# The last product of each scan block: from one VectorE instruction out of PSUM to a ScalarE copy and a GpSimd product

## The chip, the cores and the metric

The kernel runs on one core of a Trainium2 chip. The time is device microseconds (us) of one execution; three runs of the kernel before gave 946.91, 949.45 and 950.11, so their median is 949.45. A separate execution was profiled: 943.15 us, of which 941.0 lie between its first and its last instruction (the span). TensorE (PE) multiplies matrices into banks of PSUM; VectorE (DVE), ScalarE (ACT) and GpSimd (POOL) work elementwise; SyncE (SP) issues most of the DMAs. Each engine takes its own instructions in order.

## The reference

The computation is four layers, each normalised and added to x. Only the first, a Mamba block, matters here, and in it the lines from the scan to the output:

```python
def step(state, inp):
    dt_t, B_t, C_t, u_t = inp
    dA = jnp.exp(dt_t[..., None] * A)
    state = state * dA + (dt_t * u_t)[..., None] * B_t[:, None, :]
    y = jnp.einsum('bdn,bn->bd', state, C_t)
    return (state, y)
...
y = ys.transpose(1, 0, 2) + x * D
y = y * jax.nn.silu(gate)
return y @ W_out.T
```

There are 2 batches, 512 positions, 1024 channels and 16 states per channel. Then come a feed-forward layer with 4-bit weights, an attention layer and a mixture layer.

## The kernel before

The channels lie on the partitions, 128 at a time, and time runs along the free dimension. So there are 16 **blocks** (batch b, channel group c; `order[k]` in L1067), each a 128x512 tile in every quantity. A block takes 8 **steps**, one for each pair of states (`gi`); the main loop (L1152) runs over 128 steps `s = 8k + gi` and three more to drain. In step s:

- ScalarE computes the decays of step s+2 (`exps`, L1076) into one of two PSUM tiles `das`, which is free once the scan of step s has read it;
- VectorE forms du times B for step s+1 (`times_B`, L1092) and runs the recurrence of step s (`scan`, L1096);
- GpSimd multiplies the states with C (`times_C`, L1102) and, in 16 of the steps of batch 1, adds the pair up (L1104);
- TensorE adds the products of step s-2 into the bank of y (`sums`, L1124), with the identity as weights. The first matmul of a block (L1119, `gi == 0`, run in the step with gi = 2 of the next count) starts the bank with u times D.

The pool `ps_y` has one bank (L685), so y of the next block begins only when y of this one has been read. The reading is `fin(k)` (L1127), called at the head of the step with gi = 2 of the next block, that is s = 8k + 10: one VectorE product of the gate tile `g` with y, in place in `g`.

The same stage also carries other work as generators. `stream()` yields TensorE's matmuls one by one into what is free of 3.5 us per step: the gates, the in-projection of batch 1, then `out_tiles` (L978), which multiplies the finished `g` of batch 0 with W_out and starts when `st["fin7"]` is set, then the feed-forward layer of batch 0 (`ffn0`). In the steps with gi = 2 the stream's part comes before the sums, otherwise mostly after. Jobs started with `spawn(job, lag)` run in one of two `tick()`s per step; a job that puts a large product on GpSimd first takes `pool_turn()` (L181), of which there is one per step. The Softplus that makes dt of the next block (`dt_job`, L573) runs as such a job in the second tick of the step with gi = 1, ahead of that step's exps.

`pin()` (L407), called at the end of every step, fixes the order of instructions on TensorE, ScalarE, VectorE and GpSimd to the order in which they were traced. SyncE's queue is not pinned so. `jrow` hands out 128x512 tiles in SBUF from three slots. After the stage come the output projection of batch 1 (L1213) and the unpacking of the last weights (`once`).

Of the kernel before, what the change touches and what calls it, by code (L numbers as in the profile page):

```python
# [56 lines left out]
def tile_sandwich(  # L57
# [5 lines left out]
    nc = tc.nc  # L63
# [114 lines left out]
    scans, now = [], [0]  # L178
    pool_at = [-9]

    def pool_turn():  # L181

        while pool_at[0] == (now[0] - 1) // 2:
            yield 1
        pool_at[0] = (now[0] - 1) // 2
# [242 lines left out]
    with ExitStack() as mamba:  # L428
# [15 lines left out]
        def jrow(name):  # L444
            return jp.tile([P, S], F32, tag="j", name=name)
# [8 lines left out]
        g = [[None] * NCH for _ in range(B)]  # L454
# [13 lines left out]
        st = {}  # L468
# [214 lines left out]
        with ExitStack() as p2:  # L683
# [24 lines left out]
            def spawn(gen, lag=0):  # L708
                jobs.append([now[0] + lag, gen])
# [417 lines left out]
            def fin(k):  # L1127

                b, c = order[k]
                nc.vector.tensor_mul(g[b][c], g[b][c], st["y"])  # L1130
                st[f"fin{k}"] = now[0]

            def dt_job(k, ps):
                dt_out(*order[k], ps)
# [17 lines left out]
            for s in range(NS + 3):  # L1152
                k, gi = divmod(s, NGI)
# [3 lines left out]
                if gi == 2 and k:  # L1157
                    fin(k - 1)
# [39 lines left out]
        with ExitStack() as p3:  # L1198
# [9 lines left out]
            for j in range(NCH // 2):  # L1208
                w = wo_pair(1, 0, j)
                for e in range(2):  # L1210
                    c = 2 * j + e
# [305 lines left out]
```

## Time and profile before

| what | value |
|---|---|
| median of three runs | 949.45 us |
| profiled execution | 943.15 us |
| its span | 941.0 us |
| scan stage (steps 0 to 127) | about 66 to 567 us of the span |
| C product L1102, GpSimd, 128x1024 | 2362 ns, x128 |
| scan L1096, VectorE, 128x1024 | 2279 ns, x128 |
| B product L1092, VectorE, 128x1024 | 1205 ns, x127 |
| exps L1076, ScalarE, 128x511 | 691 ns, x256 |
| product of `fin` L1130, VectorE, 128x512 from PSUM | 666 ns, x16 |
| silu's product L727, GpSimd, 128x512 | 1269 ns, x15 for the gates |
| copy of dt L1084, ScalarE, 128x512 | 579 ns, x15 |
| load of an activation table, ScalarE | 1283 ns |

In a profile's groups each line names the source line, the engine, the operation, its output and inputs, their shapes, how often, the busy time with the mean of one, and after the bar the idle time just before, with the releaser that ended most of it. In a timeline the columns are start, duration, engine, line, operation and operands; in brackets stand the idle time before it and the releaser. Rows of busy time by stretch give the stretch, its length, busy time and number of records of each engine, TensorE's granted clock, the DMA share and GB/s. A matmul of fp32 operands, 128x512, shows as two records.

### The profile page before, as it was taken

What the parts mean: (1) busy time and instruction counts of PE and PEld (TensorE: products, weight loads), DVE (VectorE), ACT (ScalarE), POOL (GpSimd) and SP (SyncE); (2) the same over time, 40 slices, a digit from 0 to 9 for tenths busy, and PEclk for the clock granted to TensorE, in tenths of its full rate; (3) what the DMA queues carried; (4) which work ended last, traced back from release to release, by engine and by line L of the source; (5) the groups of instructions that cost most, each with busy time, mean ns of one, the idle gap of its engine ahead of it and who ended that gap; (6) DMA issues with size and microseconds to landing.
All of it is one profiled execution on the core that took longest, in us unless ns stands there. A gap on an engine that the chain in (4) does not pass through costs nothing.

```text
span 941.0 us, 7171 instructions
## 1 busy us (share of the span) xinstructions
PE 860.5 (91%) x2188; PEld 385.9 (41%) x2188; DVE 669.7 (71%) x770; ACT 428.3 (46%) x654; POOL 486.1 (52%) x356
## 2 busy tenths in 40 slices
PE   6989979879999898699999989899999998999994
PEld 3434433323544343244444434344544444445441
DVE  5778999999999998999999995525600034535235
ACT  3368875665667645656666530215320014322122
POOL 7758887767887777777788884520000000011012
PEclk9989999989999999799999999999999999999998
DMA  6549100110004954101110022356223121200101
GB/s 196 207 136 373 37 35 31 38 38 23 23 25 158 300 161 157 40 1 45 45 45 24 16 68 101 128 143 201 59 64 90 59 90 45 67 12 24 55 0 45
DMA packets 43816, 80.08 MB, mean 85 GB/s; under 512 B 7774, under 2 KB 20937, under 8 KB 43778
## 3 DMA queue, kind: packets, MB, share of 16 engines
q1 hardware_dynamic: 41506, 73.64, 24.0%
q0 software_dynamic: 1984, 5.47, 1.6%
q10 hardware_dynamic: 288, 0.52, 0.2%
q8 instruction: 17, 0.28, 0.1%
q14 instruction: 21, 0.17, 0.1%
HBM read 68.37 MB, written 11.24 MB: 85 GB/s over the span
## 4 chain that ended last, share of the span: by engine, by line
PE 40%; DVE 29%; issue 12%; DMA 5%; POOL 5%; ACT 3%; SPq 1%; DVEq 0%; POOLq 0%; ACTq 0%
DVE bx L1096 11%; DVE bx L1092 8%; PE pd L1445 6%; PE py L1124 5%; PE pup L1382 5%; PE fg L373 4%; PE fu L373 4%; PE fo L1298 3%; DMA B<-scr 2%; PE po L990 2%; DVE u L485 2%; PE fo L1235 2%; PE pr L1413 1%; POOL bx L1102 1%; PE pg L749 1%
## 5 line engine op out<-in xcount | busy, mean ns | idle before, releaser
L1102 POOL TENSOR_TENSOR bx<-bx,C 128x1024 f32<-128x1024 f32 x128 | 302.2, 2362 | 105.0 <-DVE bx L1096 77.9
L1096 DVE TENSOR_TENSOR_SCAN bx<-da,bx 128x1024 f32<-128x1024 f32 x128 | 291.7, 2279 | 0.3 <-ACT da L1076 0.2
L1124 PE MATMUL py<-bx,ident 128*128 128x512 f32 x480 | 234.5, 619 | 25.4 <-POOL bx L1102 21.8
L1076 ACT ACTIVATE da<-dt,A 128x511 f32<-128x511 f32 x256 | 176.5, 691 | 141.4 <-DVE bx L1096 136.8
L1092 DVE TENSOR_TENSOR bx<-du,B 128x1024 f32<-128x1024 f32 x127 | 152.9, 1205 | 3.8 <-POOL bx L1104 1.2
L1124 PEld LDWEIGHTS py<-bx,ident 128*128 128x128 f32 x480 | 91.9, 197 | 150.2 <-issue 97.3
L387 POOL TENSOR_TENSOR sd<-ve,half 128x4 f16<-128x4 f16 x2 | 2.1, 1042 | 113.1 <-DVE ve L385 113.1
L1311 DVE TENSOR_TENSOR it<-it,fu 128x512 f32<-128x512 f32 (+1 forms) x11 | 7.6, 687 | 73.6 <-PE fu L373 73.6
L749 PE MATMUL pg<-xT,w_g 128*128 128x512 f32 x114 | 56.3, 624 | 0.7 <-ACT dt L573 0.7
L1382 PE MATMUL pup<-hT_l,wup 128*128 128x512 f32 x128 | 56.2, 593 | 0.0
L1445 PE MATMUL pd<-wdn,hid 128*128 128x512 f32 x128 | 55.3, 593 | 0.0
L129 POOL TENSOR_TENSOR rs_lo<-ve_lo,mhalf 128x1 f32<-128x1 f32 x8 | 5.4, 680 | 76.7 <-DVE ve_lo L127 76.7
L1235 PE MATMUL fo<-wd,it 128*128 128x512 f32 (+1 forms) x88 | 40.0, 616 | 3.6 <-DMA wd<-wd_d 3.6
L1021 PE MATMUL fg<-hT_f,wg 128*128 128x512 f32 (+1 forms) x88 | 42.5, 594 | 0.0
L373 PE MATMUL fg<-hT_f,wg 128*128 128x512 f32 (+1 forms) x88 | 41.9, 615 | 0.7 <-ACT hT_f L173 0.7
L485 DVE SCALAR_TENSOR_TENSOR u<-px,ch,u 128x511 f32<-128x511 f32 (+2 forms) x48 | 35.9, 747 | 8.3 <-ACT u L478 7.1
L1021 PE MATMUL fu<-hT_f,wu 128*128 128x512 f32 (+1 forms) x88 | 40.4, 594 | 1.4 <-ACT dt L573 1.4
L373 PE MATMUL fu<-hT_f,wu 128*128 128x512 f32 (+1 forms) x88 | 39.8, 593 | 0.0
L1298 PE MATMUL fo<-wd,it 128*128 128x512 f32 (+1 forms) x88 | 39.6, 592 | 0.0
L1445 PEld LDWEIGHTS pd<-wdn,hid 128*128 128x128 f32 x128 | 24.2, 190 | 30.7 <-issue 30.1
L1310 ACT ACTIVATE it<-fg 128x512 f32<-128x512 f32 (+1 forms) x11 | 6.6, 597 | 65.7 <-PE fg L373 65.7
L1382 PEld LDWEIGHTS pup<-hT_l,wup 128*128 128x128 f32 x128 | 23.9, 190 | 28.2 <-issue 28.2
(243 smaller groups left out, 1168.2 us busy)
## 6 DMA issues: line engine op xcount, KB each, us to landing
wo<-in_W_outT SPq DMA_DIRECT2D x20, 512.0 KB
B<-scr SPq DMA_DIRECT2D x16, 512.0 KB
C<-scr SPq DMA_DIRECT2D x16, 512.0 KB
wg<-wgu_d SPq DMA_DIRECT2D x10, 512.0 KB
wu<-wgu_d SPq DMA_DIRECT2D x10, 512.0 KB
w_x<-in_W_in SPq DMA_DIRECT2D x8, 512.0 KB
wgu_d<-w_gu POOLq DMA_DIRECT2D x16, 256.0 KB, 2.4
w_g<-in_W_in SPq DMA_DIRECT2D x8, 512.0 KB
```

Of the source, the lines that this page charges most:

```text
L373: nc.tensor.matmul(ps[:m], w[:, kc, e * P : e * P + m], hT[:, kc, :], start=(kc == 0), stop=(kc == KH - 1),)
L749: nc.tensor.matmul(ps, w[:, k, ts(e, P)], xT[b][:, k, :], start=(k == 0), stop=(k == KH - 1))
L1021: nc.tensor.matmul(ps[:m], wt[j][a][:, kc, e * P : e * P + m], hT[:, kc, :], start=(kc == 0), stop=(kc == KH - 1),)
L1076: nc.scalar.activation(das[s % 2][:, i, 1:], st["dt", b, c][:, 1:], AF.Exp, scale=A[:, c, n : n + 1])
L1092: nc.vector.tensor_mul(bx, st["du"].unsqueeze(1).to_broadcast([P, NG, S]), Bbs[b][gi])
L1096: nc.vector.tensor_tensor_scan(flat, das[s % 2].rearrange("p n t -> p (n t)"), flat, 0.0, ALU.mult, ALU.add)
L1102: nc.gpsimd.tensor_mul(bxs[s], bxs[s], Cbs[b][s % NGI])
L1124: nc.tensor.matmul(st["y"], ident, bx[:, i, :], start=False, stop=last)
L1235: nc.tensor.matmul(fo[t], its[i][:m, ts(t, P)], w[:m, e], start=(i == 0), stop=(i == len(IC) - 1),)
L1298: nc.tensor.matmul(fo[t], its[i][:m, ts(t, P)], w[:m], start=(i == 0), stop=(i == len(IC) - 1),)
L1382: nc.tensor.matmul(ps, w[:, kc, ts(e, P)], src[kc], start=(kc == 0), stop=(kc == KH - 1))
L1445: nc.tensor.matmul(pd, hid[kc][:, ts(i, P)], wdn[kc], start=(kc == 0), stop=(kc == INT // P - 1),)
```

## The change

`fin(k)` no longer multiplies on VectorE. ScalarE copies y from its bank into a tile of `jrow` at the same place in the trace. The product of `g` with that tile goes to GpSimd, in a job that is spawned with a lag of one tick and waits for its pool turn. The note that the block is finished, `st["fin{k}"]`, is set in that job and no longer in `fin` itself.

```diff
             def fin(k):
 
                 b, c = order[k]
-                nc.vector.tensor_mul(g[b][c], g[b][c], st["y"])
-                st[f"fin{k}"] = now[0]
+                y = jrow(f"y{b}_{c}")
+                nc.scalar.copy(y, st["y"])
+
+                def times_gate():
+                    yield from pool_turn()
+                    nc.gpsimd.tensor_mul(g[b][c], g[b][c], y)
+                    st[f"fin{k}"] = now[0]
+
+                spawn(times_gate(), 1)
```

## The prediction

> **What bounds the kernel now.** I read the page's engine row and slices first, then the groups, then busy times by stretch, then the releasers of the changed line, then the timeline around one of its instances.
>
> ```profile
> PE 860.5 (91%) x2188; PEld 385.9 (41%) x2188; DVE 669.7 (71%) x770; ACT 428.3 (46%) x654; POOL 486.1 (52%) x356
> PE   6989979879999898699999989899999998999994
> DVE  5778999999999998999999995525600034535235
> ```
>
> VectorE is at nines from the fourth to the twenty-fourth slice (23.5 us each): the scan stage, about 80 to 565 us. The change lies wholly inside it. TensorE shows nines there too, but its records overlap, so I count them: back to back they start 0.43 us apart (four in 1.72 us).
>
> ```profile
> core 0: us, PE busy (x) PEld busy (x) DVE busy (x) ACT busy (x) POOL busy (x), PEclk, DMA share, GB/s
> 422.00:451.10 29.10, 28.41 (x66) 12.18 (x65) 28.97 (x21) 17.85 (x28) 21.29 (x10) 1.00 0.13 37
> 451.10:480.20 29.10, 29.10 (x68) 12.56 (x67) 29.00 (x21) 17.89 (x28) 23.79 (x13) 1.00 0.13 36
> 480.20:509.30 29.10, 28.64 (x66) 12.10 (x65) 29.00 (x21) 17.89 (x28) 23.77 (x13) 1.00 0.13 37
> ```
>
> Each row is one block of eight steps. VectorE fills 29.0 of 29.1 us, and TensorE issues 66 to 68 records x 0.43 = 28.4 to 29.2 us: **both** are full. ScalarE (17.9) and GpSimd (21 to 24) are not. From 240 to 297 us TensorE is back to back as well, by its timeline. From 103 to 236 us it holds 24 to 29 us of records per block of 28 to 37 us, so there VectorE alone sets the pace.
>
> ```profile
> L1130 DVE TENSOR_TENSOR g<-g,py x16: 659/661/689, 105.2 to 569.4; 128x512 f32<-128x512 f32 x16
>   PE py L1124: 9.3, 3
>   PEld py L1119: 16.8, 8
>   PE py L1119: 11.1, 6
> ```
>
> The product costs 0.66 us, sixteen times. VectorE stood before it for 9.3 us. Next, what matters more: L1119 (the first matmul of the next block's y) waits for it, 11.1 us in six cases, because y has one bank.
>
> **The change part by part.**
>
> *Removed from VectorE.* Fifteen products of 0.66 us inside the stage: 9.9 us. Two waits for y go from VectorE as well, 1.12 us at 268.5 and 3.42 at 359.9: 4.5 us. The third (4.74 us at 569.4) frees nothing: VectorE's next work (L201) needs a load issued only at 567.72, after TensorE's last sums. Ceiling of the gain: 14.4 us.
>
> *Added to ScalarE.* Sixteen copies; the near row is the 128x512 copy L1084, 579 ns: 9.3 us. ScalarE has 11 us idle per block, so the length is hidden. Its place is not. The copy is traced at the head of step gi=2, behind the exps that end step gi=1, and those lie behind the Softplus and two table loads:
>
> ```profile
> 452.42 1.28 ACT L573 ACT_TABLE_LOAD   x1
> 452.63 1.12 PE L568 MATMUL pv<-dtT,wdt 33*128 33x512 f32 x2
> 453.69 1.98 PE L1021 MATMUL fg<-hT_f,wg 128*128 128x512 f32 x4
> 453.79 0.60 ACT L573 ACTIVATE dt<-pv 128x512 f32<-128x512 f32 x1
> 454.18 0.66 DVE L1130 TENSOR_TENSOR g<-g,py 128x512 f32<-128x512 f32 x1
> 454.41 1.28 ACT L1076 ACT_TABLE_LOAD   x1
> ...
> 455.51 1.02 PE L1119 MATMUL py<-u,dg 128*128 128x512 f32 x2
> ...
> 455.70 1.42 ACT L1076 ACTIVATE da<-dt,A 128x511 f32<-128x511 f32 x2
> ```
>
> The bank is free at 454.84 today; y itself was complete before 453.7. With the copy it is free at 455.70 + 1.42 + 0.57 = 457.7, and TensorE, which arrives at 455.51, stands 2.1 us. The delay renews itself: if TensorE is late, pv (L568) is late, and with it Softplus, table load, exps and copy. The same reading at every boundary k (block k ends; step 8k+10), as copy end minus TensorE's arrival: k=0: 108.4-105.9 = 2.5; 2: 176.2-171.8 = 4.4; 3: 211.6-206.9 = 4.7; 4: 243.9-239.7 = 4.1 (the Softplus is followed by a gate's three activations); 5: 273.4-271.3 = 2.1; 6: 300.9-298.1 = 2.7; 9: 1.4; 10: 0.3; 11: 2.1; 12: 2.7; 13: 0.3. At 1, 7, 8 and 14 TensorE comes later than the copy would. Sum 27 us; it counts only where TensorE has no slack.
>
> *Added to GpSimd.* Sixteen products of SBUF operands; the near row is L727, the same shape, 1269 ns: 20.3 us. In the stage GpSimd is busy 378 of 481 us, and a step's own product (2.36 us of about 3.4) leaves 1.0 us. So the next C product starts 0.2 us late, 1.3 where L1104 falls in the same step (boundaries 7, 8, 11 to 14), recovered in one or two steps; its sums are due two steps later. I take 0; without that cover 6 x 1.3 = 8 us. The pool turn lets one such job in per step: at seven of the sixteen boundaries a silu or a word of the weights has it, and one of the two moves a step. No queue waits for either there: 0, bounds -2 and +2.
>
> *Port.* The Trainium skill (SBUF — State Buffer, Who interferes with whom) says that a VectorE instruction with two SBUF inputs, or in a two-port mode, is blocked by a GpSimd one that reads SBUF. The scan and the B product read one SBUF operand and show no spread (2.28 and 1.20 us). The nibble step L235 does: 0.32 us alone, 2.22 at 134.44, beside a C product at 134.11. By the rule the new product can hold only the eight nibbles and the copies of the tail. That nibble ends when GpSimd lets go, so the 0.66 of k=1 is not gained. In the tail, up to 1.3 us; I take 0.
>
> *A rule against the change.* The skill (GPSIMD Engine Reference, Engine selection; VectorE: DVE Perf Modes, Rules for kernel authors) gives a two-input product to VectorE, GpSimd being about twice as slow, and would copy out of PSUM only for several uses. The rows agree on price: 1.27 + 0.57 against 0.66 us. Paid in series that is 16 x 1.18 = +19 us; by the rows both are in engines with room, so I charge nothing for length, only the bank's later release.
>
> *fin7.* out_tiles starts at the step in which fin7 is set. It was set before TensorE's part of step 66, now in that step's tick, so W_out's matmuls start in step 67. TensorE held them from 327.48, the load's landing, to 334.4; it would stand until the copy at about 330.1: 2.6 us. The consumers move a step too; I take +2 (0 to 3.5).
>
> **The sum,** against the profiled execution (span 941.0, total 943.15):
>
> - k=0 to 3: at 0, TensorE 2.5 us late holds the gate's activation at 115.84, thus exps to 121.2 where scan 14 began at 120.44: +0.8. k=1: 0; k=2, 3: -0.66 each (TensorE has 8 us of slack per block). Together -0.5.
> - k=4 to 6: TensorE +4.1 - 0.5 = 3.6, then 2.1: 5.7 us late, with nothing to catch up in, since ScalarE already waits for it:
>
> ```profile
> 283.19 0.60 ACT L722 ACTIVATE th<-pg 128x512 f32<-128x512 f32 x1 [2.57 <-PE pg L749]
> ```
>
>  The du copy and exps follow this activation, and VectorE waited for du at 286.63 already, so the stage stands at +5.8. k=6: the stall falls into some 4 us of slack; -0.7. Now +5.1.
> - k=7, 8: -0.66, then -0.66 - 3.42 as VectorE no longer waits for y; +2 for fin7. Now +2.4.
> - k=9 to 14: TensorE adds 1.4 + 0.3 + 2.1 + 2.7 + 0.3 = 6.8 against 1.9 us of TensorE's idle time in those blocks (0.69 + 0.69 + 0.46): +4.9. Now +7.3; -0.66 at k=14 and up to 2.1 (VectorE's wait for GpSimd before the last up product, which moves past the last scan): +4.8.
>
> 943.15 + 4.8 = 948.0. That execution is 6.3 us under the median 949.45; the same step on the median gives **954.3 us**.
>
> **Rivals.**
>
> 1. *VectorE alone decides.* For: its 97% of the stage. If TensorE's queued matmuls outlast the copy at each boundary, the gain stands: 9 x 0.66 = 5.9 for k=0 to 8, 4.5 of waits, nothing where TensorE is full: -10.4, 939.1. It decides once the copy's end comes before TensorE's arrival, as at 1, 7, 8, 14. Against: eleven of fifteen boundaries do not look so. 20%.
> 2. *It cancels.* The slack absorbs half of the stalls (TensorE in part waits for other things anyway): 949.5. 20%.
> 3. *GpSimd becomes the bound.* If the 1.3 us at the six crowded steps passes to sums and bx buffers, +8 on my sum: 962. For: TensorE waited 25.3 us for GpSimd before L1124 already. Against: six bx buffers, and sums two steps behind. 15%.
>
> That y's copy and product do what they say I take as given: the near rows name both operations.
>
> **Numbers.** My forecast 45%, own range 951 to 959. Range for all 943 to 964, leaving out half of rival 1 and the far end of 3. About 0.3% (2.9 us) is what can be told from no change. Slower: nearly all of mine, 3: 0.58. Same: rival 2 and my low edge: 0.21. Faster: rival 1: 0.21.
>
> **What would show it.** Right: L1119 waits for the ScalarE copy, some 20 us in all, 2 us or more at k=4, 5, 11, 12; VectorE idle in 240 to 300 and 450 to 510 us where it had none; scan stage 4 to 6 us longer. Wrong: L1119's waits near 11 us and VectorE still at 99% (rival 1); waits of L1124 for GpSimd well over 25 us (rival 3).

## The result, and the profile after

The changed kernel takes **958.11 us** (median of 6 runs, 951.97 to 964.5), the kernel before 948.65 (6 runs beside it, 946.91 to 950.11): a ratio of 1.0098, 95% interval 1.0073 to 1.0123. That is slower by 9.5 us. The forecast was +4.8 us, 954.3.

The two profiled executions lie further apart than the medians: 960.53 us after, 943.15 before. Each is a single execution, one above its median and one below. So I take places from the profiles, and sizes from medians.

From the page of after, first the engines and VectorE's slices, then two groups:

```profile
PE 866.7 (90%) x2188; PEld 389.5 (41%) x2188; DVE 660.3 (69%) x754; ACT 436.5 (46%) x670; POOL 505.3 (53%) x372
DVE  5778987999989898998999995544420025625225
...
L1096 DVE TENSOR_TENSOR_SCAN bx<-da,bx 128x1024 f32<-128x1024 f32 x128 | 291.7, 2280 | 10.4 <-ACT da L1076 10.3
...
L1119 PE MATMUL py<-u,dg 128*128 128x512 f32 x32 | 22.6, 795 | 33.2 <-ACT y L1131 33.2
```

The work moved as written: VectorE has 16 instructions fewer, ScalarE and GpSimd 16 more each, at the durations forecast (0.578 and 1.27 us). But VectorE's row of nines has holes now: the scan waits 10.3 us for decays from ScalarE, where it waited 0.2 before:

```profile
L1096 DVE TENSOR_TENSOR_SCAN bx<-da,bx 128x1024 f32<-128x1024 f32 x128 | 291.7, 2279 | 0.3 <-ACT da L1076 0.2
```

And L1119, which starts each block's y, waits 33.2 us where it waited 11.1. Who waits for the copy is in the answer for its line (microseconds, then times):

```profile
L1131 ACT COPY y<-py x16: 577/578/587, 109.9 to 587.0; 128x512 f32<-128x512 f32 x16
...
  PEld py L1119: 42.2, 13
  PE py L1119: 33.2, 11
  POOL g L1135: 10.1, 5
```

One such boundary, k=2, in the timeline (before, the same L1119 started at 171.82 after 3.09 us of waiting for VectorE):

```profile
179.92 1.28 ACT L573 ACT_TABLE_LOAD   x1
...
181.22 0.60 ACT L573 ACTIVATE dt<-pv 128x512 f32<-128x512 f32 x1
181.83 1.28 ACT L1076 ACT_TABLE_LOAD   x1
...
183.12 1.41 ACT L1076 ACTIVATE da<-dt,A 128x511 f32<-128x511 f32 x2
...
184.47 0.58 ACT L1131 COPY y<-py 128x512 f32<-128x512 f32 x1
...
185.10 2.08 PE L1119 MATMUL py<-u,dg 128*128 128x512 f32 x2 [7.48 <-ACT y L1131]
...
187.83 0.34 PEld L1124 LDWEIGHTS py<-bx,ident 128*128 128x128 f32 x1 [0.52 <-issue]
188.68 0.34 PEld L1124 LDWEIGHTS py<-bx,ident 128*128 128x128 f32 x1 [0.52 <-issue]
...
190.60 0.19 PEld L1124 LDWEIGHTS py<-bx,ident 128*128 128x128 f32 x1 [0.24 <-issue]
191.03 0.19 PEld L1124 LDWEIGHTS py<-bx,ident 128*128 128x128 f32 x1 [0.24 <-issue]
```

The copy itself is 0.58 us. It comes last in a queue of 4.6 us: table load, Softplus, table load, exps; ScalarE had worked without a gap since 176.80. TensorE stands for 7.48 us, and the last four lines show a second price: the weight loads after the stall take 0.34 us and start 0.85 us apart, and only some four us later 0.19 and 0.43. TensorE restarts at half its clock. Busy time by stretch shows it; the last number but two of a row is the granted clock:

```profile
177.60:178.80 1.20, 0.03 (x1) 0.00 (x0) 1.20 (x2) 1.20 (x3) 1.20 (x1) 1.00 0.02 7
178.80:185.10 6.30, 0.00 (x0) 0.00 (x0) 6.14 (x5) 6.18 (x9) 6.30 (x5) 0.50 0.23 82
185.10:189.10 4.00, 4.00 (x5) 1.85 (x6) 3.27 (x4) 1.90 (x3) 2.15 (x2) 0.50 0.00 0
189.10:193.00 3.90, 3.90 (x10) 1.71 (x9) 3.90 (x3) 2.62 (x6) 2.58 (x2) 1.00 0.00 0
```

The Trainium skill (TensorE: Matmul & The Clock Gate, Part 1) describes this: after an idle window of some 3.4 us the clock is halved until about as long a stretch of work. The trace agrees on the halving and on the stretch of work, 4.0 us here. It does not agree on what goes before: the clock was halved 1.2 us after TensorE's last matmul had ended.

### The profile page after: what moved, and what is told of

Same layout as the page of the kernel before. It is cut to its first block, busy times and chain, and to the rows that moved or that the text cites. A ratio compares the mean times of both kernels' runs of the same rounds, so it can differ in the third digit from the quotient of the medians.

```text
span 958.7 us, 7210 instructions
## 1 busy us (share of the span) xinstructions
PE 866.7 (90%) x2188; PEld 389.5 (41%) x2188; DVE 660.3 (69%) x754; ACT 436.5 (46%) x670; POOL 505.3 (53%) x372
## 4 chain that ended last, share of the span: by engine, by line
PE 56%; DVE 14%; ACT 9%; POOL 7%; issue 5%; DMA 2%; SPq 1%; POOLq 0%; DVEq 0%; ACTq 0%
PE py L1124 13%; PE pd L1452 6%; DVE bx L1096 6%; PE pup L1389 5%; PE fg L373 4%; PE fu L373 4%; PE fo L1305 3%; PE fu L1021 3%; PE pg L749 3%; PE fg L1021 3%; POOL bx L1102 3%; ACT da L1076 3%; PE po L990 2%; DVE bx L1092 2%; PE fo L1242 2%
## 5 line engine op out<-in xcount | busy, mean ns | idle before, releaser
L1102 POOL TENSOR_TENSOR bx<-bx,C 128x1024 f32<-128x1024 f32 x128 | 302.5, 2368 | 89.3 <-DVE bx L1096 78.3
L1096 DVE TENSOR_TENSOR_SCAN bx<-da,bx 128x1024 f32<-128x1024 f32 x128 | 291.7, 2280 | 10.4 <-ACT da L1076 10.3
L1124 PE MATMUL py<-bx,ident 128*128 128x512 f32 x480 | 237.3, 626 | 16.1 <-POOL bx L1102 13.4
L1124 PEld LDWEIGHTS py<-bx,ident 128*128 128x128 f32 x480 | 94.6, 201 | 140.4 <-issue 103.7
L1119 PE MATMUL py<-u,dg 128*128 128x512 f32 x32 | 22.6, 795 | 33.2 <-ACT y L1131 33.2
L485 DVE SCALAR_TENSOR_TENSOR u<-px,ch,u 128x511 f32<-128x511 f32 (+2 forms) x48 | 35.9, 747 | 16.4 <-ACT u L478 15.3
L1452 PEld LDWEIGHTS pd<-wdn,hid 128*128 128x128 f32 x128 | 24.2, 190 | 30.7 <-issue 30.1
```

Source lines behind the costliest of these rows:

```text
L1096: nc.vector.tensor_tensor_scan(flat, das[s % 2].rearrange("p n t -> p (n t)"), flat, 0.0, ALU.mult, ALU.add)
L1102: nc.gpsimd.tensor_mul(bxs[s], bxs[s], Cbs[b][s % NGI])
L1124: nc.tensor.matmul(st["y"], ident, bx[:, i, :], start=False, stop=last)
L1452: nc.tensor.matmul(pd, hid[kc][:, ts(i, P)], wdn[kc], start=(kc == 0), stop=(kc == INT // P - 1),)
```

## The experiments

Each was timed in three rounds beside the kernel before, whose median was 948.3 beside e1 to e4, 948.8 beside e5 to e8 and 948.9 beside the rest. Medians of few runs (e1, e4, e10 and e12 have four) carry intervals of 4 to 5 us to either side, the others 1.4 to 2.7.

**e1_hold: the late release alone.** The kernel before, with one more instruction:

```diff
                 nc.vector.tensor_mul(g[b][c], g[b][c], st["y"])
+                nc.scalar.copy(jrow(f"y{b}_{c}"), st["y"])
```

> The kernel before, with the ScalarE copy of y added at the place where the change has it, and nobody reading the copy: VectorE still multiplies from the bank. Only the hold on y's bank is new. Theory (the bank is freed late, behind Softplus, table load and exps on ScalarE): as slow as the change or slower, since VectorE is not relieved of its 10 us: 956 to 966, L1119 waiting some 25 to 35 us. Rival (GpSimd's product or its turn costs the time): no GpSimd work is added, so 947 to 951.

972.37 us, ratio 1.0245 (1.019 to 1.03). The direction is the theory's, the size is above it. TensorE's waits from 80 to 600 us:

```profile
PE py L1119 <- ACT y L1131: 37.8, 12, 7.8
```

Against 11.1 us in the kernel before, that is 26.7 us of added wait, for +23.6 us of time: almost nothing was absorbed. (The copy also takes ScalarE's time and a slot of `jrow`; no run adds these alone.)

**e2_dve_copy: GpSimd's product without ScalarE.** The change, with the copy on VectorE:

```diff
-                nc.scalar.copy(y, st["y"])
+                nc.vector.tensor_copy(y, st["y"])
```

> The change with the copy out of the bank on VectorE, at the old place of the product; GpSimd multiplies as in the change. The bank is freed as before, VectorE keeps about 0.66 us per block. Theory (late bank): 945 to 951, L1119 waiting about 11 us as before. Rival (GpSimd's product, its turn, or out_tiles a step later): the loss stays, 955 to 960.

947.25 us, ratio 0.9974 (0.996 to 0.9989). VectorE's copy takes 0.666 us, as much as its product did. So the product on GpSimd, with its turn and its later note, does not by itself make a kernel slower: as the bound, rival 3 falls. What it costs once VectorE is relieved is another matter (see e8 against e10, below).

**e3_early_copy: the copy ahead of the Softplus.** The change, with `fin` called one step earlier, in front of that step's first tick:

```diff
-                if gi == 2 and k:
-                    fin(k - 1)
...
+                if gi == 1 and k:
+                    fin(k - 1)
```

> The change with the copy moved up to the end of the sums of step gi=1, so that it stands on ScalarE ahead of the Softplus, the table loads and the exps of that step. Theory (place in ScalarE's queue): the stalls of L1119 fall from 33 to under 8 us and VectorE keeps its relief: 938 to 948, faster than before. Rival (GpSimd or its turn): 955 to 960, as the change.

955.83 us, ratio 1.007 (1.0051 to 1.009). L1119 waited for only 3.1 us in all, yet hardly any time came back: the waits are the theory's, the time is the rival's. The edit had moved two more things: ScalarE now stood 22.3 us for y before its copy (12.4 of them at the last block), and the note that starts the out_tiles fell into step 66 in place of 67.

**e4_fin_at_once: only the start of the out_tiles.** The change, with the note set in `fin` itself as before (step 66):

```diff
                     nc.gpsimd.tensor_mul(g[b][c], g[b][c], y)
-                    st[f"fin{k}"] = now[0]

                 spawn(times_gate(), 1)
+                st[f"fin{k}"] = now[0]
```

> The change with the note that a block is finished set at once, so that out_tiles starts in step 66 as before; copy and product as in the change. Theory (late bank): fin7 is worth 0 to 3.5 us of the loss: 954 to 958. Rival (the later start of out_tiles is the loss): 947 to 950.

968.91 us, ratio 1.0206 (1.0163 to 1.0249). Both expectations missed: the later start, which the prediction booked as a loss, had saved the change 10.8 us. The loss does not lie where the out_tiles start: from scan 66 to scan 70 e4 takes 13.25 us, the change 14.62. It lies between scan 70 and scan 126, 231.0 us against 219.1, and at the last scan, 2.5 us. Two of VectorE's waits between scans 70 and 126, in e4:

```profile
DVE it L1009 <- POOL it L727: 8.2, 3, 3.1
DVE it L1009 <- issue: 5.2, 1, 5.2
```

In the change:

```profile
DVE it L1009 <- POOL it L727: 1.8, 2, 0.9
```

L1009 is the up product of the feed-forward layer, L727 the silu's product on GpSimd that it needs. (A wait put down to "issue" is one for which the profile shows no releaser.) The start shifts all of the stream's work behind the out_tiles against the steps, and here VectorE stands before these products for longer.

**e5_dt_later: the Softplus behind the copy.** The change, with dt's job spawned one tick later:

```diff
-                                 spawn(dt_job(dt_due, dt_in(*order[dt_due])), 2)
+                                 spawn(dt_job(dt_due, dt_in(*order[dt_due])), 3)
```

> The change with the Softplus of the next block (dt_job) one tick later, so that it and its two table loads, some 3.2 us, stand on ScalarE behind the copy of y and no longer ahead of it. Theory (the bank waits for what is queued ahead of the copy): L1119's stalls fall from 33 to under 12 us and the time to 940 to 952. Rival (the time goes by the order of TensorE's stream against the steps, whatever holds the bank): 955 to 965.

**943.27 us**, ratio 0.9948 (0.992 to 0.9976), 14.8 us below the change. The same boundary k=2, in its timeline:

```profile
173.90 1.42 ACT L1076 ACTIVATE da<-dt,A 128x511 f32<-128x511 f32 x2 [3.71 <-DVE bx L1096]
...
175.25 0.58 ACT L1131 COPY y<-py 128x512 f32<-128x512 f32 x1
...
175.88 2.07 PE L1119 MATMUL py<-u,dg 128*128 128x512 f32 x2 [2.97 <-ACT y L1131]
...
179.10 1.28 ACT L573 ACT_TABLE_LOAD   x1
180.40 0.60 ACT L573 ACTIVATE dt<-pv 128x512 f32<-128x512 f32 x1
```

The copy follows the exps directly, and the two table loads come after it. This wait falls from 7.48 to 2.97 us, all of L1119's waits to 17.1. Below 12, as expected, they are not: behind the previous step's exps the copy is still later than VectorE was. The place in ScalarE's queue is confirmed as the cause of these 14.8 us.

**e6_no_product: the relief alone.** The kernel before, without VectorE's product; y is left out of the layer.

> The kernel before without the product of gate and y: fin only notes the step, nothing reads y (this leaves the multiplication by y out of layer 1). It gives the ceiling of what relieving VectorE can bring, with no hold on the bank: theory 933 to 941 (9.9 us of products, 4.5 us of waits). Rival (VectorE is not what ends these steps; TensorE is): 945 to 949.

942.93 us, ratio 0.9932 (0.9911 to 0.9952): only 5.9 us, with no reader of the bank left at all. Missed; together with e4 it pointed to the step in which the out_tiles start.

**e7_before_fin_late: the later start alone.** The kernel before, with the note set one tick later:

```diff
-                st[f"fin{k}"] = now[0]
+
+                def note():
+                    st[f"fin{k}"] = now[0]
+                    yield 1
+
+                spawn(note(), 1)
```

> The kernel before with the note that a block is finished set one tick later, so that out_tiles starts in step 67 as in the change; the product stays on VectorE. Theory (the later start helped the change only by moving the stream against the copies, whose stalls this kernel has not): 945 to 951. Rival (a start in step 67 is worth 10 us by itself): 936 to 942.

945.3 us, ratio 0.9959 (0.9943 to 0.9976). Starting in step 67 is worth 3.5 us with no other edit.

**e8_early_copy_fin_late: e3 with the start in step 67.**

```diff
                     nc.gpsimd.tensor_mul(g[b][c], g[b][c], y)
+                    yield 2
                     st[f"fin{k}"] = now[0]
```

> The early copy (ahead of the Softplus) with the note set one step later, so that out_tiles starts in step 67 as in the change. Theory (what the early copy still lost was the start in step 66, under which the late blocks' up products wait for GpSimd): 942 to 950. Rival (ScalarE's waits for y, in the early place, are the loss): 953 to 958, as the early copy alone.

944.59 us, ratio 0.9957 (0.9938 to 0.9976). So what e3 had lost, 11.2 us, it lost by the start in step 66, with hardly a stall at L1119 in either.

**e9_before_dt_later: the control for e5.** e7 with dt's job one tick later, as in e5.

> The kernel before, with VectorE's product as it was, but with the out_tiles starting in step 67 of their block (as the change has them, 945.3 us alone) and with dt's Softplus job one tick later. If the later dt only helped the change because ScalarE's copy then stood ahead of the Softplus, it has nothing to help here: 944 to 948 us, L1119's wait for VectorE near the 11 us that the start in step 67 shows alone, and 943.3 us of the change with the later dt is about 2 us of relief. Rival: the later dt is worth something by itself: 938 to 943 us, and the change with the later dt then owes it nothing else.

944.01 us, ratio 0.996 (0.9941 to 0.9979), L1119 waiting 7.3 us for VectorE. The later Softplus is worth nothing measurable to a kernel that has no copy behind it. And e5 cannot be told from e9 or e7: what it gains by VectorE's relief it loses again elsewhere. The copy's remaining delay, the copy itself and GpSimd's product are what it has more; no run separates these.

**e10_no_product_fin_late: the relief with the start in step 67.** e7 without the product; y is left out of the layer again.

> The kernel before with the out_tiles starting in step 67 and VectorE's 16 products left out (y is not read and the gate is not multiplied): the relief of VectorE in the change's own schedule, to stand beside 945.3 us with the products. If relief and later start add up (942.9 us for the relief alone, 3.5 us for the start), 938 to 941 us. Rival: both take the same wait of TensorE for VectorE away, so that there is nothing left to gain: 942 to 946 us.

931.29 us, ratio 0.9846 (0.9801 to 0.9892): 14.0 us below e7, more than either side had expected. Relief and start don't add; each makes the other worth more. The timelines of e6 and e10 show some of it. Both reach step 66 with the same spacing. First e6, where the out_tiles start in step 66:

```profile
327.02 8.01 PE L990 MATMUL po<-wo,g 128*128 128x512 f32 x12 [1.46 <-DMA wo<-in_W_outT]
...
334.88 1.02 PE L1119 MATMUL py<-u,dg 128*128 128x512 f32 x2
...
335.74 1.88 PE L1124 MATMUL py<-bx,ident 128*128 128x512 f32 x4
...
337.71 1.23 DVE L1092 TENSOR_TENSOR bx<-du,B 128x1024 f32<-128x1024 f32 x1 [2.81 <-issue]
```

Then e10:

```profile
321.37 1.12 PE L1119 MATMUL py<-u,dg 128*128 128x512 f32 x2
322.33 1.88 PE L1124 MATMUL py<-bx,ident 128*128 128x512 f32 x4
...
324.36 5.39 PE L990 MATMUL po<-wo,g 128*128 128x512 f32 x12 [0.15 <-DMA wo<-in_W_outT]
```

In step 66 TensorE waits for W_out's load and then runs twelve of its matmuls, the first six at half pace, in 8.0 us, ahead of L1119 and the sums. VectorE stops for 2.81 us and goes on as these sums end. In step 67 the sums go first, the load has landed but for 0.15 us, and the same twelve take 5.4 us. From scan 66 to scan 70 e6 loses 2.9 us on e10, up to scan 126 another 3.9 in small pieces, and 2.8 at the last scan, which an up product (L1009) precedes in e6 and follows in e10. That makes 9.5, on top of 2.5 by which the two lay apart at scan 66.

**e11_fin_at_once_dt_later: e4 with dt's job one tick later.**

> The change with out_tiles starting in step 66 (968.9 us alone) and dt's Softplus job one tick later (943.3 us alone). If the early start costs what it cost the change, about 11 us, whatever stands in ScalarE's queue: 951 to 957 us. Rival: the early start hurts only where the copy is behind the Softplus and the boundary's stall is long: 944 to 949 us, and L1119's waits for the copy below 20 us.

951.37 us, ratio 1.0022 (1.0008 to 1.0037), 8.1 us above e5; L1119 waited 20.3 us. The early start costs this kernel nearly as much, with over a third of the waits gone, so it does not need the long stalls.

**e12_hold_fin_late: e1 with the start in step 67.**

> The kernel before with ScalarE's unread copy of y added (972.4 us with the start in step 66) and the out_tiles starting in step 67. It holds the bank as the change does and keeps VectorE's product, so it differs from the change (958.1 us) by the relief and by GpSimd's product alone. If the start is worth about 11 us to a kernel with a held bank: 959 to 964 us, and the relief is worth 1 to 6 us of it. Rival: the relief is worth nothing while TensorE stalls for the bank: 956 to 959 us. Should the start be worth only the 3.5 us that it brings the kernel before: 966 to 971 us.

969.56 us, ratio 1.0237 (1.0193 to 1.028). It holds the bank as the change does; from 80 to 600 us:

```profile
PE py L1119 <- ACT y L1131: 38.0, 11, 7.5
```

To a kernel whose VectorE keeps its product the start is worth 2.8 us (the intervals of e1 and e12 leave it open within some 6) or 3.5 (e7), not 11, bank held or not. The change stands 11.5 us below this kernel: that is the relief, inside the change, less what GpSimd's product costs.

## Why: the prediction step by step

Four pairs of kernels differ in whether ScalarE, behind the Softplus, holds the bank (medians, us):

| out_tiles start in step | VectorE's product | bank free early | bank held by ScalarE | cost of holding |
|---|---|---|---|---|
| 66 | kept | 948.8 (before) | 972.4 (e1) | 23.6 |
| 66 | taken off | 942.9 (e6) | 968.9 (e4) | 26.0 |
| 67 | kept | 945.3 (e7) | 969.6 (e12) | 24.3 |
| 67 | taken off | 931.3 (e10) | 958.1 (the change) | 26.8 |

The rows "kept" measure the hold: 23.6 and 24.3. In the rows "taken off" the held kernels have ScalarE's copy and GpSimd's product as well, and the free ones neither. What these cost, e8 shows: the product taken off, the start in step 67, only 3.1 us of waits at L1119, and still 944.6 us, 13.3 above e10. In their traces 6.4 us of it lie between scan 68 and scan 84. From e8:

```profile
355.73 1.27 POOL L1135 TENSOR_TENSOR g<-g,y 128x512 f32<-128x512 f32 x1 [1.82 <-ACT y L1131]
...
361.92 0.69 DVE L121 BATCH_NORM_STATS2 st_f<-x 128x6 f32<-128x512 f32 x1 [2.26 <-POOL x L914]
```

GpSimd waits for the copy, its queue behind this product is late, and VectorE waits for it; e10 has no wait of VectorE there. So of the 26.8 us some 13.5 go when the bank is freed early, and some 13.3, give or take 5, stay with copy and product in a kernel whose VectorE is relieved.

A way through the table from before to the change is +23.6 (hold), -2.8 (start), -11.5 (relief, less GpSimd's product): +9.3. Beside it, the prediction's sum sorted in the same way:

| term | forecast | measured |
|---|---|---|
| added waits of L1119 | 27, and 2.6 at k=7 | 26.7 (e1), 26.9 (e12), 22.1 (the change) |
| their effect on the end: 0.8 (k=0) + 6.3 (k=4 to 6) + 4.9 (k=9 to 14) | +12.0 | +23.6 |
| start of the out_tiles: +2 at k=7, -1.8 at the tail | +0.2 | -2.8 (-3.5 without the hold) |
| VectorE's relief: 1.3 + 0.7 + 4.7 + 0.7 | -7.4 | -11.5 |
| sum | +4.8 | +9.3 |

The forecast came near by luck as well as by reading: the effect of the waits was 11.6 us above its term, and the start and the relief, 3.0 and 4.1 us better than booked, hid most of that.

**Right, by the boundary.** The waits were forecast from the trace of before as copy end minus start of L1119, so they come on top of what L1119 waited already. e1, which adds the hold and nothing else, gives them one by one, as its wait minus that of before: k=0 2.87 - 0.39 = 2.5 (forecast 2.5), k=2 7.48 - 3.09 = 4.4 (4.4), k=3 7.78 - 3.88 = 3.9 (4.7), k=4 5.42 - 1.64 = 3.8 (4.1), k=5 2.0 (2.1), k=6 2.88 - 0.07 = 2.8 (2.7), k=11 2.0 (2.1). In the change itself k=4 to 6 and most of the late blocks stalled less than in e1, and k=7 stalled 4.3 us, where the prediction had 2.6, in its term for the out_tiles.

**Right:** the direction; that GpSimd's length costs next to nothing where VectorE keeps its work (e2: the change with a VectorE copy is 2 us above e7, within their intervals); that the port costs next to nothing (one nibble beside the new product, at 196.82 us in the trace of after, took 0.70 us in place of 0.32). The rule that gives such a product to VectorE, weighed at +19 us if paid in series, did not decide; the queue in front of the copy did.

**The step that failed** is the netting: "k=2, 3: -0.66 each (TensorE has 8 us of slack per block)", and likewise the 4 us of slack into which k=6 was to fall. 27 us of waits were to move the end by 12; they moved it by 24, or 0.9 us for each added us in e1 and e12. The trace of after has steps 10 to 34, forecast at -0.5, 9.8 us late at scan 34, 1.5 of them since scan 10; e12 has 4.6 and e1 7.7 there.

One reason why the slack wasn't there is the clock. Three pairs of kernels are the same program through step 65: the change and e4, e1 and e12, e5 and e11. From scan 10 to scan 42, in this order: before; the change, e4; e1, e12; e5, e11:

```profile
106.94:240.73 133.79, 112.85 (x248) 45.94 (x247) 132.35 (x104) 87.81 (x134) 102.03 (x60) 0.94 0.10 35
...
108.41:250.85 142.44, 117.19 (x248) 48.90 (x248) 129.21 (x101) 89.60 (x138) 107.03 (x64) 0.87 0.08 29
108.82:245.94 137.12, 112.50 (x248) 47.23 (x248) 129.07 (x100) 89.56 (x138) 106.94 (x64) 0.91 0.09 30
...
107.65:249.55 141.90, 116.51 (x248) 49.08 (x248) 132.63 (x105) 88.67 (x137) 102.02 (x60) 0.87 0.10 33
107.09:245.34 138.25, 112.88 (x248) 47.56 (x248) 132.41 (x104) 88.77 (x137) 101.93 (x60) 0.90 0.10 34
...
105.43:241.95 136.52, 113.39 (x237) 47.58 (x238) 129.31 (x100) 87.97 (x135) 106.35 (x63) 0.87 0.08 30
106.18:237.95 131.77, 108.91 (x237) 46.06 (x238) 129.51 (x101) 88.02 (x135) 106.41 (x63) 0.91 0.09 31
```

Within a pair L1119's four waits in this stretch are within 0.7 us of each other (18.5 and 17.8; 18.1 and 17.6; 12.5 and 12.5) and TensorE's records are as many. The one with the lower granted clock has 3.6 to 4.7 us more of busy TensorE and takes 3.7 to 5.3 us longer. So at the same stalls the time goes with the granted clock, and that differs from one execution to the next. The six runs of the change say it too, from 951.97 us at a clock of 0.960 to 964.5 at 0.946. The prediction counted the slack in records of 0.43 us, which is the full clock. But a low clock is not all: e5 has 0.87 here, as the change has, and ends 14.8 us earlier.

The second reason is the way the lateness takes, which the prediction described for k=0 and 4 but not for k=1 to 3: late matmuls of pg and px hold the activations behind them, those the exps, and the exps the scan. In the trace of after VectorE's idle time before its L485 at 149.91 us is 5.81, waiting for an activation that waited 3.25 us for px. How much of the 24 us of the whole stage is the clock and how much this chain, no run separates.

**The sign that failed** is fin7. The prediction saw W_out's load and the late L1119 of that block, and left out that in step 66 the out_tiles stand ahead of the block's sums, in step 67 behind them, and that all later work of the stream moves with them. Six pairs differ in the start alone. Where VectorE keeps its product it was worth 3.5 us (before, e7) and 2.8 (e1, e12); where it does not, 11.6 (e6, e10), 10.8 (e4, the change), 11.2 (e3, e8) and 8.1 (e11, e5). In the traces 2.5 to 2.8 us of it fall at the last scan in every pair; the prediction had this gain, at 1.8 us, and took it for one of relief. The order against the sums costs 2.9 us between scans 66 and 70 in e6 and 1.3 in before, and nothing in e3, e4 and e11, which lose 7.3 to 11.9 us between scans 70 and 126. Why the start matters more once VectorE is relieved stays open; e4's waits of L1009 show one place.

**Rivals.** 1 (VectorE alone decides, 939.1): the relief of 14.4 us exists, as e10's 14.0, but only with the bank free and the later start. 2 (cancels): no. 3 (GpSimd): not as the bound that was forecast, though e8 against e10 leaves it a share that no run isolates. TensorE's wait for GpSimd's C products (L1102) fell from 21.8 us to 13.4 in the change. In e2 it was 30.1, which the prediction would have taken for a sign of this rival; but it was 34.1 in e10, the fastest of all, which gives GpSimd nothing more to do; so that sign does not tell the rivals apart. At the tail the forecast held: the last up product went past the last scan, and the scan's lag on the trace of before falls from 18.9 us at scan 126 to 16.1 at 127.

**A version that beats both** is e5, 943.3 us, one digit away from the change; e7, e8 and e9, at 944.0 to 945.3, can't be told from it. The 931.3 us of e10 show what a kernel could reach that frees the bank early and takes the product off VectorE; a second bank for y was not tried.

## What to carry to other kernels

When an operation that frees a single buffer moves to another engine, price what stands ahead of it in that engine's queue, not its own length: a copy of 0.58 us per block cost some 24 here, and one tick in the order of the Softplus took 14.8 back. Count the waits of an engine that is over 90% busy at nearly their full length on the end, unless the trace shows the work that it would catch up in. And when an edit moves a flag, look at what the flagged work will stand ahead of in the queues, and at all that moves with it.

## What was not expected of the hardware

TensorE's half-paced restart did not need a long stall in this kernel: in the trace of after the pair of L1119 takes 1.02 us without a stall and 2.08 after 2.31 us of waiting at k=9 (1.34 after 2.01 at k=10); before, 2.07 after 1.64 at k=4. So the length of the wait alone doesn't tell which clock follows; what else decides, no run here shows.
